# Local attention layers: where the shifted copies of the values are issued, and which engine writes their column of ones

## The chip, the core and the metric

The kernel runs on one core of a Trainium2 chip. Five engines are named in what follows: TensorE (PE for its matmuls, PEld for its weight loads), VectorE (DVE), ScalarE (ACT), GpSimd (POOL), and SyncE (SP), which here does nothing but issue DMAs, in the order of the program. The metric is the time of one execution on the device in microseconds (us).

## What is computed

A small transformer over x of 4 x 512 x 128: cross-attention and feed-forward layers before and after, and between them a stack of six local layers, which is where the change lies. One of them, cut to what matters:

```python
qkv = x @ Wqkv                       # 16 heads of 64
q = l2norm(q) * qs; k = l2norm(k) * ksc
q = q * cos * scale + rotate_half(q) * sin * scale      # k with 1 / scale
# windows of 32 rows: each looks at its own 32 keys and the 32 before
bk2 = concatenate([previous window of k, window of k])
bv2 = concatenate([previous window of v, window of v])
sim = q @ bk2.T * 8, masked to the 33 keys i-32 .. i
out = softmax(sim) @ bv2
x = out @ Wo + x
x = feed_forward(shift_tokens(x)) + x
```

## The kernel before

**Tiles and periods.** The local stack (`local_transformer`) works on tiles of 128 tokens: 6 layers x 4 rows x 4 tiles = 96 tiles. One loop, `for n in range(len(tiles) + 2)`, runs over periods. The order of every engine's instructions is that of the program (a manual schedule), and in period n three tiles are in work: T = tile n (its queries, keys and values), T1 = tile n-1 (transposes, scores, softmax) and T2 = tile n-2 (average, output projection). Every four periods a row of the feed-forward layer is woven in as well, in four phases.

The order within a period, with the lines that the profile names:

1. At n = 7, 23, 39, 55, 71 the next layer's weights are loaded: twelve DMAs on SP (`local_columns` L1757 to L1761, `local_weights` L1769 to L1781). At n = 4, once, two buffers in HBM are cleared for the last layer: POOL fills a tile (L527, L528), then SP issues three DMAs (L533 twice, L537), some 2 MB each.
2. Products of queries and keys on TensorE (L1842), their squares on ScalarE (L1844); `rotate` on VectorE (L1852, L1855, and the sum of squares L1864), with an addition on POOL (L1865). Between them the transposes of T2's probabilities (L621, copied by L1970), the first feed-forward part (L2017, L2028, L2039), the averages of T2 (`average`, L1980, twice), T1's transposes (L621, L1896), and T2's division (L1989, L1990).
3. The scores of T1 (L1940, L1949).
4. The last `rotate`; `normalise` of T on POOL (L1875 to L1884, the last of which are four products of 128x512); `softmax` of T1: row maxima on VectorE (L1959), subtraction (L1960), exponential on ScalarE (L1965).
5. The output projection of T2 (L2004) and the residual (L2011); in the first feed-forward phase the layer norm on VectorE (`ff_norm`, L559), whose result L2028 transposes in the next period.
6. `values` of T: products (L1919), copied to `v1` by ScalarE (L1920).
7. The second feed-forward part (L2039, L2050, L2062).

**v1 and v2.** `average` multiplies with 65 columns: 64 values and a column of ones that gives the sum of the probabilities. A window's 64 keys are its own 32 and the 32 before; windows of odd number find them as 64 neighbouring partitions of `v1`, those of even number in `v2`, a copy of `v1` shifted by 32 partitions (`x0` tells even and odd heads, whose halves lie swapped). Six DMAs within SBUF make `v2` (L1922 to L1930; four for the first tile of a row, whose missing part POOL sets to zero at L1915, L1916); two of them take rows of the tile before. The DMAs move the column of ones too, so they stand behind the memset that writes it, L1913 on POOL, which in POOL's order stands behind the four products of `normalise`. `v1` and `v2` have three buffers each.

In period n the copies of tile n go out; `average` reads them in period n+2.

Of the kernel before, what the change touches and what calls it, by code (L numbers as in the profile page):

```python
# [35 lines left out]
DEPTH, LH, LD, WIN = 6, 16, 64, 32  # L36
# [87 lines left out]
def bc(ap, shape, *axes):  # L124

    for a in axes:
        ap = ap.unsqueeze(a)
    return ap.to_broadcast(shape)
# [144 lines left out]
def tile_kernel(ctx: ExitStack, tc: tile.TileContext, A: dict, out: bass.AP):  # L273
    nc = tc.nc
    V, G, SC, PE, DMA = nc.vector, nc.gpsimd, nc.scalar, nc.tensor, nc.sync
# [43 lines left out]
    def p_tr(*shape):  # L319
        return psum(shape, "tr", 2)  # L320
# [199 lines left out]
    def clear(pool, i):  # L520


        t = pool.tile([128, NT, D], F32, name="xn")
        t = t.rearrange("p a b -> p (a b)")[:, : 2 * ROW].rearrange("p (a b) -> p a b", b=ROW)

        def fill(e):
            e.memset(t, 0.0)  # L527
            e.memset(t[:, 1, D + 1 :], NOWHERE)  # L528

        def send(e):  # L530
            for j in (1, 2) if i else (0,):
                r = sent[j].rearrange("(c p) d -> p c d", p=128)
                e.dma_start(r, bc(t[:, int(j != 1)], [128, r.shape[1], ROW], 1))  # L533

        def send_back(e):
            r = back[i].rearrange("(c p) d -> p c d", p=128)
            e.dma_start(r, bc(t[:, 0, :D], [128, 2 * NTT, D], 1))  # L537

        return fill, send, send_back
# [1211 lines left out]
    def local_columns(i, wp):  # L1751

        W = A["L2_ffn_Wqkv"][i]
        w = []
        for j in range(4):
            t = wp.tile([128, 512], F32, name="wqk", bufs=8)
            DMA.dma_start(t, W[:, 512 * j : 512 * j + 512])  # L1757
            w.append(t)
        qs = wp.tile([128, 2, LD], F32, name="qs", bufs=1)
        DMA.dma_start(qs[:, 0], A["L2_ffn_q_scale"][i].partition_broadcast(128))  # L1760
        DMA.dma_start(qs[:, 1], A["L2_ffn_k_scale"][i].partition_broadcast(128))  # L1761
        return w, qs

    def local_weights(i, wp, lf):

        W = A["L2_ffn_Wqkv"][i]
        wv = wp.tile([128, 2, 512], F32, name="wv")
        for x0 in range(2):
            DMA.dma_start(  # L1769
                wv[:, x0].rearrange("p (k d) -> p k d", d=LD),  # L1770
                W[:, 2 * INNER :].rearrange("p (k x d) -> p x k d", x=2, d=LD)[:, x0],
            )
        wo = wp.tile([128, 8, D], F32, name="wo")
        DMA.dma_start(wo, A["L2_ffn_Wo"][i].rearrange("(c p) d -> p c d", p=128))
        w1 = lf.tile([128, 2 * DI], F32, name="lw1")
        DMA.dma_start(w1, A["L2_ffn_W1"][i])
        w2 = lf.tile([128, 3, D], F32, name="lw2")
        DMA.dma_start(
            w2[:, 0:2], A["L2_ffn_W2"][i][0:256].rearrange("(c p) d -> p c d", p=128)
        )  # L1780
        DMA.dma_start(w2[: CH_W[2], 2], A["L2_ffn_W2"][i][256:DI])  # L1781
        return wv, wo, w1, w2
# [21 lines left out]
    def local_transformer(Y, lf, lw, columns, tabs):  # L1804

        with ExitStack() as es:
# [98 lines left out]
            def values(T, x0):  # L1905

                b, tt = T.b, T.tt
                if x0 == 0:  # L1910
                    T.v1 = vp.tile([128, 2, LH // 2, LD + 1], F32, name="v1")
                    T.v2 = vp.tile([128, 2, LH // 2, LD + 1], F32, name="v2")
                    G.memset(T.v1[:, :, :, LD : LD + 1], 1.0)  # L1913
                    if tt == 0:
                        G.memset(T.v2[0:32, 0], 0.0)  # L1915
                        G.memset(T.v2[64:96, 1], 0.0)  # L1916
                t = p_tr(128, 8, LD)
                src = Y[b] if x0 == 0 else swapped[b]
                PE.matmul(t, src[:, 128 * tt : 128 * tt + 128], T.wv[:, x0], start=True, stop=True)  # L1919
                SC.copy(T.v1[:, x0, :, 0:LD], t)  # L1920
                if x0 == 0:
                    DMA.dma_start(T.v2[32:128, 0], T.v1[0:96, 0])  # L1922
                    if tt:
                        DMA.dma_start(T.v2[0:32, 0], T.before.v1[96:128, 0])
                else:
                    DMA.dma_start(T.v2[96:128, 1], T.v1[64:96, 1])
                    DMA.dma_start(T.v2[0:32, 1], T.v1[96:128, 1])
                    DMA.dma_start(T.v2[32:64, 1], T.v1[0:32, 1])
                    if tt:
                        DMA.dma_start(T.v2[64:96, 1], T.before.v1[32:64, 1])  # L1930

            def scores(T):

# [21 lines left out]
            def softmax(T):  # L1955

                P = tp.tile([128, LH // 2, 2, LD], F32, name="P", bufs=1)
                mx = small.tile([128, 2, LH // 2], F32, name="la_mx")
                V.tensor_reduce(mx, T.banks, AX.X, ALU.max)  # L1959
                V.tensor_tensor(  # L1960
                    P.rearrange("p k z d -> p z k d"), T.banks,
                    bc(mx, [128, 2, LH // 2, LD], 3), ALU.subtract,
                )
                T.P = P.rearrange("p k z d -> p k (z d)")
                SC.activation(T.P, T.P, AF.Exp, scale=8.0)  # L1965

            def probabilities(T):
                T.PT = tp.tile([128, LH // 2, 128], F32, name="PT", bufs=1)
                for g in range(2):
                    SC.copy(T.PT[:, 4 * g : 4 * g + 4], to_features(T.P[:, 4 * g : 4 * g + 4]))  # L1970
# [51 lines left out]
            def ff_norm(F):  # L2022
                layernorm(F.xn, F.xn, F.found)
# [71 lines left out]
            for n in range(len(tiles) + 2):  # L2095
                T = tiles[n] if n < len(tiles) else None
                T1 = tiles[n - 1] if 0 <= n - 1 < len(tiles) else None
                T2 = tiles[n - 2] if 0 <= n - 2 < len(tiles) else None
                m, phase = divmod(n - 6, 4)
                F = rows[m] if 0 <= m < len(rows) else None  # L2100
                if T:
                    if n % 16 == 7 and T.i + 1 < DEPTH:
                        columns[T.i + 1] = local_columns(T.i + 1, lw)
                        loaded[T.i + 1] = local_weights(T.i + 1, wp, lf)
                    if n == 4:
                        fill, send, send_back = clear(lnp, 1)
                        fill(G)
                        send(DMA)
                        send_back(DMA)
                    if n % 16 == 15 and T.i + 1 < DEPTH:  # L2110
                        tabs[T.i + 1] = local_tables(columns[T.i + 1][1], lw)
                    T.before = tiles[n - 1] if T.tt else None
                    T.w, (T.wv, T.wo) = columns[T.i][0], loaded[T.i][:2]
                    T.tabs = tabs[T.i]
                    queries_or_keys(T, 0, 0)
                if T2:
                    probabilities(T2)
                if T:
                    queries_or_keys(T, 0, 1)
                    rotate(T, 0, 0)  # L2120
                if F:
                    ff_stage(F, phase, False)
                if T2:
                    average(T2, 0)
                if T1:
                    turned(T1, 0)
                if T:
                    queries_or_keys(T, 1, 0)
                if T2:
                    normalised(T2, 0)  # L2130
                if T:
                    rotate(T, 0, 1)
                if T2:
                    average(T2, 1)
                if T1:
                    turned(T1, 1)
                if T:
                    queries_or_keys(T, 1, 1)
                if T2:
                    normalised(T2, 1)  # L2140
                if T:
                    rotate(T, 1, 0)
                if T2:
                    attended(T2)
                if T and T.tt == NT - 1 and n + 1 < len(tiles):
                    swap(tiles[n + 1].b)
                if T1:
                    scores(T1)
                if T:
                    rotate(T, 1, 1)  # L2150
                if T:
                    normalise(T)
                if T1:
                    softmax(T1)
                if T2:
                    project_out(T2)
                    residual(T2)
                if F and phase == 0:
                    ff_norm(F)
                if T:  # L2160
                    values(T, 0)
                    values(T, 1)
                if F:
                    ff_stage(F, phase, True)
# [134 lines left out]
```

## Time and profile before

| | us |
|---|---|
| three runs, median | 2462.2 (2459.23 to 2467.07) |
| the profiled execution | 2456.04 |
| its span | 2454.2 |
| local layers, within the span (first and last average) | 545 to 2164 |
| TensorE busy | 2228.0 |
| VectorE busy | 1759.3 |
| GpSimd busy | 1338.6 |
| ScalarE busy | 1298.1 |

All statements of durations come from the profiled execution; 1.8 us of its time lie outside the span. Rows of a timeline have the start and the duration in us, the engine, the line, the operation and what it writes and reads; a bracket at the end has the engine's idle time before it and what ended it. SPq is SP's queue, where the duration is that of issuing, not of the transfer. A busy TensorE isn't a TensorE at its peak, and what an engine waits for is inferred from semaphores.

### The profile page before, as it was taken

The numbers are of one execution on the slowest core, as the hardware profiler recorded it, in microseconds if no ns is written. First come the engines' busy times: TensorE is split into PE (matmuls) and PEld (weight loads), VectorE is DVE, ScalarE is ACT, GpSimd is POOL, SyncE is SP. The second block draws the span as 40 slices with busy tenths as digits, with TensorE's granted clock in tenths as the row PEclk, the third lists the DMA queues.
The fourth block names the chain that finished last, engine by engine and source line by source line (L and its number), as shares of the span: only waits on it lengthen the run. The fifth ranks groups of instructions, "written<-read, shape, count | busy, mean of one in ns | idle before, by whom it ended". The sixth has DMA issues, their size and how long they took to land. (4 is left out here: it accounts for less than half of the span.)

```text
span 2454.2 us, 86703 instructions
## 1 busy us (share of the span) xinstructions
PE 2228.0 (91%) x37341; PEld 1479.5 (60%) x37341; DVE 1759.3 (72%) x3896; ACT 1298.1 (53%) x2389; POOL 1338.6 (55%) x1862
## 2 busy tenths in 40 slices
PE   7958969978999999999999999999999999989676
PEld 3536734546666666666666666666666666644355
DVE  5545356866888888777887888887878788767422
ACT  3423325645666655666666666565666666525222
POOL 2141330256667676766667766766667666710433
PEclk9868989988999999999999999999999999989688
DMA  7201110016211121111211121111211111120023
GB/s 182 68 21 41 40 60 2 1 41 135 80 35 29 35 70 36 33 29 35 75 31 36 29 79 33 29 35 27 80 31 31 35 29 35 27 67 23 26 67 95
DMA packets 134298, 116.14 MB, mean 47 GB/s; under 512 B 29506, under 2 KB 102701, under 8 KB 133917
## 3 DMA queue, kind: packets, MB, share of 16 engines
q1 hardware_dynamic: 122037, 99.67, 15.8%
q0 software_dynamic: 4608, 7.35, 0.9%
q8 instruction: 296, 4.85, 0.9%
q10 hardware_dynamic: 7271, 3.58, 0.5%
q14 instruction: 86, 0.70, 0.1%
HBM read 42.84 MB, written 21.52 MB: 26 GB/s over the span
## 5 line engine op out<-in xcount | busy, mean ns | idle before, releaser
L1865 POOL TENSOR_TENSOR rc<-rc,rs 128x512 f32<-128x512 f32 x384 | 489.8, 1276 | 400.7 <-DVE rs L1855 326.3
L1842 PE MATMUL ps_mm<-wqk,y 128*128 128x512 f32 x768 | 397.2, 599 | 5.3 <-issue 3.5
L1884 POOL TENSOR_TENSOR rc<-rc,rn_y 128x512 f32<-128x512 f32 x384 | 388.6, 1044 | 7.5
L1852 DVE TENSOR_TENSOR rc<-ps_mm,tabs 128x512 f32<-128x512 f32 x384 | 262.5, 684 | 129.8 <-ACT sq L1844 126.5
L1844 ACT ACTIVATE sq<-ps_mm 128x512 f32<-128x512 f32 x384 | 231.2, 602 | 161.4 <-PE ps_mm L1842 108.0
L1855 DVE TENSOR_TENSOR rs<-ps_mm,tabs 128x512 f32<-128x512 f32 x384 | 261.5, 681 | 0.2 <-POOL rc L1865 0.2
L1864 DVE TENSOR_REDUCE ss<-sq 128x8 f32<-128x512 f32 x384 | 259.5, 676 | 0.0
L621 PE MATMUL ps_tr<-cst,rc 128*128 128x128 f32 x1536 | 210.9, 280 | 4.3 <-POOL rc L1884 4.0
L1980 PEld LDWEIGHTS ps_av<-v,PT 64*32 64x32 f32 x12288 | 138.1, 105 | 126.5 <-PE ps_tr L621 54.1
L2004 PE MATMUL ps_av<-aT,wo 128*128 128x128 f32 x1536 | 200.7, 283 | 2.4 <-issue 2.4
L2004 PEld LDWEIGHTS ps_av<-aT,wo 128*128 128x128 f32 x1536 | 181.0, 193 | 12.6 <-issue 3.9
L621 PEld LDWEIGHTS ps_tr<-cst,rc 128*128 128x128 f32 x1536 | 165.6, 142 | 24.4 <-POOL rc L1884 5.1
L1949 PE MATMUL ps_sc<-kT,qT 64*32 64x64 f32 x12288 | 148.1, 225 | 33.6 <-issue 32.9
L1980 PE MATMUL ps_av<-v,PT 64*32 64x65 f32 x12288 | 170.3, 225 | 6.2 <-DVE attn L1990 1.7
L1949 PEld LDWEIGHTS ps_sc<-kT,qT 64*32 64x32 f32 x12288 | 141.2, 105 | 44.2 <-issue 38.1
L1056 POOL DMA_INDIRECT back<-ye,to x80 | 78.8, 985 | 147.5 <-DVE ye L1170 104.0
L1842 PEld LDWEIGHTS ps_mm<-wqk,y 128*128 128x128 f32 x768 | 124.5, 192 | 56.3 <-issue 50.1
L1965 ACT ACTIVATE P<-P 128x1024 f32<-128x1024 f32 x96 | 101.4, 1057 | 97.3 <-DVE P L1960 97.3
L1876 ACT ACTIVATE rn_y<-ss 128x32 f32<-128x32 f32 x96 | 22.0, 229 | 237.9 <-POOL ss L1875 237.9
L802 ACT ACTIVATE P<-ps,deltaT 77x512 f32<-77x512 f32 x192 | 115.8, 683 | 56.7 <-PE ps L796 53.0
L1896 ACT COPY qT<-ps_tr 128x512 f32<-128x512 f32 x192 | 103.3, 589 | 74.6 <-PE ps_tr L621 74.3
L1959 DVE TENSOR_REDUCE la_mx<-ps_sc 128x16 f32<-128x1024 f32 x96 | 116.9, 1218 | 31.0 <-PE ps_sc L1949 31.0
(399 smaller groups left out, 4368.9 us busy)
## 6 DMA issues: line engine op xcount, KB each, us to landing
v<-v SPq DMA_DIRECT2D x432, 65.0 KB
v<-v SPq DMA_DIRECT2D x96, 195.0 KB
wqk<-in_L_ffn_Wqkv_dram SPq DMA_DIRECT2D x24, 256.0 KB
sent<-xn SPq DMA_DIRECT2D x2, 2210.0 KB
xe<-sent SPq DMA_DIRECT2D x16, 260.0 KB
back<-xn SPq DMA_DIRECT2D x2, 2048.0 KB
raw<-in_L_ffn_W_dram SPq DMA_DIRECT2D x8, 512.0 KB
w<-in_L_ffn_W_dram SPq DMA_DIRECT2D x16, 256.0 KB
```

Source lines behind the costliest of these rows:

```text
L621: PE.transpose(t[:, i], src[:, i], ident)
L1842: PE.matmul(t, lhs, T.w[2 * kind + c], start=True, stop=True)
L1844: SC.activation(sq, t, AF.Square)
L1852: V.tensor_tensor(a, t, bc(T.tabs[:, 2 * kind, tt], [128, 8, LD], 1), ALU.mult)
L1855: V.tensor_tensor(r.rearrange("p h (x d) -> p h x d", x=2), t.rearrange("p h (x d) -> p h x d", x=2)[:, :, ::-1], bc(T.tabs[:, 2 * kind + ...
L1864: V.tensor_reduce(T.ss[:, kind, 8 * c : 8 * c + 8], sq, AX.X, ALU.add)
L1865: G.tensor_tensor(a, a, r, ALU.add)
L1884: G.tensor_tensor(a, a, bc(y[:, o : o + 8], [128, 8, LD], 2), ALU.mult)
L1949: PE.matmul(T.banks[32 * w : 32 * w + 32, z, k], T.qT[r, k, 32 * w : 32 * w + 32], T.kT[r, k, 32 * w : 32 * w + 64], start=False, stop=Tru ...
L1959: V.tensor_reduce(mx, T.banks, AX.X, ALU.max)
L1980: PE.matmul(T.means[32 * w : 32 * w + 32, x0, k], T.PT[r, 4 * g + k, 32 * w : 32 * w + 32], (T.v1 if w % 2 else T.v2)[r, x0, 4 * g + k], s ...
L2004: PE.matmul(t, T.wo[:, c], T.aT[:, c], start=(c == 0), stop=(c == 7))
```

## The change

The function `ship` takes the six DMAs out of `values`, and in front of them the column of ones is written by VectorE instead of POOL. It is called for T1 just ahead of its `softmax`: the copies of tile n now go out in period n+1, in step 4 above. `average` still reads them in period n+2. On VectorE the memset stands behind the last `rotate` and ahead of the row maxima. On SP the copies of tile n-1 now stand behind the DMAs that step 1 of period n issues. Shapes and transfers are the same.

```diff
@@ values(T, x0)
                 if x0 == 0:
                     T.v1 = vp.tile([128, 2, LH // 2, LD + 1], F32, name="v1")
                     T.v2 = vp.tile([128, 2, LH // 2, LD + 1], F32, name="v2")
-                    G.memset(T.v1[:, :, :, LD : LD + 1], 1.0)
                     if tt == 0:
                         G.memset(T.v2[0:32, 0], 0.0)
                         G.memset(T.v2[64:96, 1], 0.0)
...
                 SC.copy(T.v1[:, x0, :, 0:LD], t)
-                if x0 == 0:
-                    DMA.dma_start(T.v2[32:128, 0], T.v1[0:96, 0])
-                    if tt:
-                        DMA.dma_start(T.v2[0:32, 0], T.before.v1[96:128, 0])
-                else:
-                    DMA.dma_start(T.v2[96:128, 1], T.v1[64:96, 1])
-                    DMA.dma_start(T.v2[0:32, 1], T.v1[96:128, 1])
-                    DMA.dma_start(T.v2[32:64, 1], T.v1[0:32, 1])
-                    if tt:
-                        DMA.dma_start(T.v2[64:96, 1], T.before.v1[32:64, 1])
+            def ship(T):
+
+                v1, v2 = T.v1, T.v2
+                before = T.before.v1 if T.tt else None
+                V.memset(v1[:, :, :, LD : LD + 1], 1.0)
+                DMA.dma_start(v2[32:128, 0], v1[0:96, 0])
+                if T.tt:
+                    DMA.dma_start(v2[0:32, 0], before[96:128, 0])
+                DMA.dma_start(v2[96:128, 1], v1[64:96, 1])
+                DMA.dma_start(v2[0:32, 1], v1[96:128, 1])
+                DMA.dma_start(v2[32:64, 1], v1[0:32, 1])
+                if T.tt:
+                    DMA.dma_start(v2[64:96, 1], before[32:64, 1])
@@ the loop over periods
                 if T:
                     normalise(T)
                 if T1:
+                    ship(T1)
                     softmax(T1)
                 if T2:
                     project_out(T2)
```

## The prediction

> **What bounds the kernel now.** I read the page first, then the local stretch alone, then who waits in it, then one period of the loop, and last the one place where the sync queue (SP) carries something big.
>
> ```profile
> PE 2228.0 (91%) x37341; PEld 1479.5 (60%) x37341; DVE 1759.3 (72%) x3896; ACT 1298.1 (53%) x2389; POOL 1338.6 (55%) x1862
> PE   7958969978999999999999999999999999989676
> 700.00:2100.00 1400.00, 1360.74 (x27239) 923.36 (x27239) 1140.44 (x1991) 857.36 (x1565) 957.02 (x1344) 1.00 0.15 40
> PE ps_sc L1949 <- issue: 26.1, 26, 1.5
> PE ps_tr L621 <- ACT v L1920: 3.4, 12, 0.3
> PE ps_sc L2028 <- DVE xn L559: 3.0, 8, 0.5
> ```
>
> Lines one and two are the page's; the third is the window table (us, then busy time of PE, PEld, DVE, ACT, POOL, clock, DMA share, GB/s); the last three are TensorE's waits in that window (total us, times, longest). TensorE is busy 1360.7 of 1400 us, and two thirds of the 39 us that are missing are "issue" before the scores, which no engine and no copy ends. No wait on the copies of v appears. So nothing that is merely taken off POOL or SP can help; what can happen is a new wait. One period lasts about 17 us (82 row maxima, L1959, in 1400 us).
>
> **How much room the copies have.** Timeline of a period with the least room, and a set of copies:
>
> ```profile
> 1030.62 0.68 DVE L1864 TENSOR_REDUCE ss<-sq 128x8 f32<-128x512 f32 x1
> 1031.21 1.22 DVE L1959 TENSOR_REDUCE la_mx<-ps_sc 128x16 f32<-128x1024 f32 x1
> ...
> 1037.96 1.02 PE L1980 MATMUL ps_av<-v,PT 64*32 64x65 f32 x64
> ...
> 1038.51 0.13 POOL L1913 MEMSET v<- 128x16 f32 x1
> 1038.66 0.53 SPq L1922 DMA_DIRECT2D v<-v  x1
> ```
>
> Now the copies of tile n go out behind POOL's memset at 1038.66, and are read over a period later. After the change they go out just before L1959 of the next period (1031.21 here), and the average L1980 at 1037.96 reads them: 6.75 us. What a set needs: from the first issue at 1019.33 to the last, L1930, 1022.47 + 0.59 = 1023.06, that is 3.73 us of issuing; the window table has the DMA share at 0.05 in 1024.0 to 1024.5 and 0.00 after, so 5.2 us at most. The slowest ordinary set, from 1038.66, still moves in 1044 to 1045: 6.3 us. Other tiles have 8 to 10 us (1013.16 to 1022.35, 1047.46 to 1056.22). So ordinary copies arrive in time, with 0.4 to 1.5 us to spare in every fourth tile. I cost this at nothing; the upper end is 24 tiles x 0.5 us = 12.
>
> **The SP queue that the copies are moved past.** SP works in order. At 7, 23, 39, 55 and 71, weight loads stand at the head of a period, and at 4 the clearing of the buffers in HBM (L533, L537). Today both stand behind the copies that are next needed; afterwards the copies of tile n-1 stand behind them.
>
> ```profile
> 579.16 0.59 SPq L1930 DMA_DIRECT2D v<-v  x1
> 579.86 8.05 SPq L533 DMA_DIRECT2D sent<-xn  x2
> 587.96 12.94 SPq L537 DMA_DIRECT2D back<-xn  x1
> 601.01 9.16 SPq L1922 DMA_DIRECT2D v<-v  x1
> ...
> 588.53 0.42 PE L1980 MATMUL ps_av<-v,PT 64*32 64x65 f32 x21
> 597.60 1.22 PE L1842 MATMUL ps_mm<-wqk,y 128*128 128x512 f32 x1 [3.50 <-issue]
> ```
>
> ```profile
> 588.00:596.00 8.00, 5.76 (x149) 3.62 (x147) 6.77 (x13) 3.83 (x7) 6.71 (x9) 1.00 1.27 190
> 596.00:604.00 8.00, 5.49 (x127) 4.01 (x128) 1.88 (x3) 2.23 (x5) 2.40 (x6) 0.55 1.29 180
> 604.00:610.00 6.00, 3.92 (x34) 3.74 (x34) 2.45 (x2) 0.78 (x1) 4.59 (x7) 0.50 1.14 306
> ```
>
> The clearing holds SP and all DMA engines from 579.86 to 610.17 (601.01 + 9.16, when the copy behind it was taken). It already costs something: TensorE waits for instructions, its clock falls to 0.5, and the row maxima of tiles 3 and 4 lie 24.2 us apart (582.50, 606.70). The L1930 above is tile 3's, and tile 3 is averaged at 588.53.
>
> **Part by part.**
>
> *Clearing, once.* Afterwards tile 3's six copies are issued in period 4 behind the clearing. SP gets to it when POOL's fill ends (L528, 575.34) less the memset that goes, 0.13: 575.21, that is 4.65 us earlier than 579.86. The first copy is then taken at 610.17 - 4.65 = 605.52; five more take 3.73 - 0.53 = 3.2; the last lands 1.0 to 1.4 us after its issue (1023.06 to 1024.0 or 1024.5): 610.0. The average that ran at 588.53 waits until then: 21.5 us of new wait on TensorE, with everything else of the period queued behind it. Average to maxima took 8.11 us in the period before (574.39 to 582.50). The clock will be low after such a gap: at best nothing is lost, at worst all 8.11 us of it run at half speed; in the rows it stayed near 0.5 from 596.8 to 610.4 after a gap of 3.5 us, but with gaps inside. I take 2.5 us. The maxima of tile 4 come at 610.0 + 8.1 + 2.5 = 620.6 instead of 606.70. Part comes back: the instruction starvation is hidden in the wait (counted already, since 606.70 holds it), and the next period, 17.30 us (606.70 to 624.00), holds a slow L2004 (3.78 us where 2.05 is usual), 1.7 us. I take half of that: 16.5. So 637.1 against 624.00: **+13.1 us**; ends +9.7 (no cold loss, all 1.7 back, 609.6) and +18.
>
> The Trainium skill, "TensorE: Matmul & The Clock Gate", Part 1, says that the array is cold after an idle window of about 3.4 us and warm again after about 3.4 us of steady work. By that rule the cold loss would be about 1.7 us instead of my 2.5, and the sum 0.8 us lower; the 13.6 us at 0.5 in this trace had further gaps in them.
>
> *Weight loads, five times.* Their issues take 635.91 to 645.74. Afterwards they start when tile 5's copies are issued (maxima at 624.00, so near 628) and are issued by 638, before the maxima of tile 6 at 640.27: the copies find SP free. Zero, up to 1 us each; 0 to +5.
>
> *Ones on VectorE.* VectorE's memsets cost 60 ns for 77x2 (L658) and 485 ns for 128x512 (L654), on one line with 16 elements at 72 ns: 96 x 0.072 = 6.9 us. It stands behind L1864 and ahead of L1959; behind it wait the maxima, the subtraction, the residual and, every fourth period, the norm L559, on which TensorE's L2028 waits. In 30 of 96 periods VectorE waits for the scores anyway (31.0 us). Where TensorE waits for VectorE's chain it is one period in four: 24 x 0.072 = **+1.7 us**; elsewhere TensorE's own work covers it.
>
> A worse price is possible: L559 beside POOL's L1884 takes 957 ns, the same kind of operation and size (L588) 348. If POOL's addition L1865, in flight at that moment, held the memset as well, it would be 0.6 us each, 14 us in 24 periods, 58 in all. Rows L654 and L658 are memsets and read nothing; I take them.
>
> The Trainium skill, "SBUF — State Buffer", "Who interferes with whom", lists copies, casts and tensor_scalar as holders of the port that VectorE shares with GpSimd, and says that an instruction with at most one SBUF input outside those modes doesn't contend. By it the memset pays nothing extra, and the 0.6 us would be no case at all; no row here has a VectorE memset beside a busy POOL.
>
> *Removed from POOL.* 96 x 128 ns = 12.3 us, behind the norm's four products and ahead of L1865, which waits 326 us for VectorE anyway; nothing waits on POOL's memset but SP. Zero.
>
> *DMA out of the averages' way.* TensorE's "issue" waits at L1980 and L621 are 1.6 us in the window: 0 to -2; I take 0.
>
> Sum: 13.1 + 1.7 = **+14.8 us**, on the profiled execution's 2456.04: 2470.8. The three runs' median is 6.2 us higher, 2462.2, so I forecast 2477.0. A change under 0.3% (7.4 us) can't be told from none here.
>
> **Rivals.**
> 1. *The clearing is hidden (not slower).* The present kernel loses 7 us there already; if the copies land soon enough, the wait only replaces that. With tile 3's copies landing at 597 instead of 610 the 13.1 is gone. For it: the clearing's first two transfers are issued in 8 us. Against: L1922 sat 9.16 us. Time 2462 to 2466. Chance 0.13.
> 2. *Copies late throughout, or a memset that blocks.* 24 tiles x 0.5 = 12, or 24 x 0.6 = 14, weights 5: +27 to +32 in all, 2489 to 2494. For it: a margin of 0.4 us; against: rows above. Chance 0.17.
> 3. *Faster.* If the "issue" gaps before the scores (26.1 in 1400, 30 in the whole stage) were due to the copies' packets, their going would outweigh the clearing: 14.8 - 30 = -15, 2447. It decides from about 15 us saved. Against: the packets are over by 1024.5 and the scores run at 1029. Chance 0.06.
> 4. *Nothing moves*, because the copies still go out as before: impossible to see in the rows; in 1.
>
> Forecast 0.64. Slower by over 0.3%: 0.64 + 0.17 = 0.81; within: 0.13; faster: 0.06. The range goes from 2464 (rival 1, upper part) to 2494 (rival 2).
>
> **What will show it.** Right: L1980 with one wait of some 20 us on a DMA of v near 588, tile 3's L1922 behind L537, maxima of tiles 3 and 4 some 38 us apart, MEMSET on DVE near 72 ns, no other DMA wait in 700 to 2100. Wrong: L1980 waiting in many periods, a MEMSET far over 0.1 us, or less "issue" time before L1949.

## The result, and the profile after

Five runs of the changed kernel have a median of 2486.8 us (2484.0 to 2488.7) against 2462.2 us before: a ratio of 1.0098, with a 95% interval of 1.0082 to 1.0114. The change makes the kernel 24.6 us slower; the forecast was 14.8 us slower, within a range that holds the measured time. The profiled execution took 2484.23 us, its span 2482.2.

TensorE's line and its slices on the page after:

```profile
PE 2236.2 (90%) x37341; PEld 1483.3 (60%) x37341; DVE 1761.5 (71%) x3992; ACT 1297.6 (52%) x2389; POOL 1330.6 (54%) x1766
PE   7958969977999999999999999999999999989676
```

TensorE does the same work, with one slice at 7 where there was an 8. TensorE's waits after, in 560 to 2164 us (total us, times, longest):

```profile
PE ps_sc L1951 <- issue: 36.0, 31, 3.1
PE ps_av L1982 <- DMA v<-v: 15.1, 2, 14.9
PE ps_av L1982 <- issue: 6.2, 5, 2.2
PE ps_tr L621 <- POOL kT L1892: 2.2, 1, 2.2
```

and the same before:

```profile
PE ps_sc L1949 <- issue: 32.9, 31, 2.2
PE ps_av L1980 <- issue: 1.7, 4, 0.6
```

(In the kernel after, the scores L1949 are L1951, the averages L1980 L1982, the maxima L1959 L1961, and the copies L1925 to L1932.) Two things are new and recur below: one wait of 14.9 us for a copy of v, and waits for instructions ("issue") at the averages. The single wait of 2.2 us at L621, put down to POOL, lies in the fifth weight load (at 1749.92 us).

The plainest ruler is the row maxima, one per tile: they give the length of every step. In the table, "all" runs from the maxima of tile 0 to those of tile 95, "2 to 5" covers the clearing, "5 to 6" is the sum of the five steps between tiles 5 and 6 of layers 0 to 4 (the steps after which the next layer's weights must be under way), and "rest" is what remains. Each figure is a difference of starts of that line in one profiled execution, in us.

| | all | 2 to 5 | 5 to 6, five | rest |
|---|---|---|---|---|
| before | 1615.4 | 56.5 | 80.5 | 1478.4 |
| after | 1636.0 | 67.5 | 93.3 | 1475.2 |

The stage is 20.6 us longer: 11.0 at the clearing, 12.8 at the five weight loads, and -3.2 in the 87 steps of the rest. In this pair of profiles another 7.4 us lie outside the stage, where the instructions are the same. That part moves from one execution to the next: the maxima of tile 0 came at 515.0, 515.7 and 518.6 us in three profiles of the experiments below, whose programs don't differ before them. 20.6 us is inside the interval of the runs (20.2 to 28.1 us).

Each figure of the table comes from one profile of each kernel, and such a figure moves too. Up to tile 5, experiment 4 below runs the same program as the kernel before and takes 51.9 us from tile 2 to 5 instead of 56.5; experiment 1 runs the same as the kernel after and takes 64.1 instead of 67.5. So the clearing's cost is 8 to 16 us, 11.0 in this pair. The rest lies between 1471.8 and 1481.3 us in all profiles but those of experiments 7 and 8, so its -3.2 is no change that can be told from none.

**The clearing.** SP and TensorE after (timeline; SPq durations are of issuing):

```profile
576.17 0.59 SPq L1932 DMA_DIRECT2D v<-v  x1
580.48 7.79 SPq L533 DMA_DIRECT2D sent<-xn  x2
588.32 12.43 SPq L537 DMA_DIRECT2D back<-xn  x1
600.86 8.76 SPq L1925 DMA_DIRECT2D v<-v  x1
...
589.85 0.97 PE L1951 MATMUL ps_sc<-kT,qT 64*32 64x64 f32 x72 [3.06 <-issue]
590.75 3.34 PE L2006 MATMUL ps_av<-aT,wo 128*128 128x128 f32 x16
613.61 0.39 PE L1982 MATMUL ps_av<-v,PT 64*32 64x65 f32 x2 [14.85 <-DMA v<-v]
```

Tile 3's first copy is taken at 600.86 + 8.76 = 609.62, its last is issued at 612.21, and the average that reads them starts at 613.61 after a wait of 14.85 us. The scores ahead of it have already waited 3.06 us for instructions, and L2006 runs at half clock (3.34 us where it takes 2.05; the window table reads 0.50 for 592 to 594 us).

**The weight loads.** The step from tile 21 to tile 22, after:

```profile
915.93 1.20 DVE L1961 TENSOR_REDUCE la_mx<-ps_sc 128x16 f32<-128x1024 f32 x1
919.85 2.04 SPq L1757 DMA_DIRECT2D wqk<-in_L_ffn_Wqkv_dram  x4
927.81 0.33 PE L1982 MATMUL ps_av<-v,PT 64*32 64x65 f32 x12 [1.57 <-issue]
928.65 0.36 SPq L1781 DMA_DIRECT2D lw<-in_L_ffn_W_dram  x1
933.93 0.65 PE L1951 MATMUL ps_sc<-kT,qT 64*32 64x64 f32 x40 [1.79 <-issue]
```

and before:

```profile
897.21 1.22 DVE L1959 TENSOR_REDUCE la_mx<-ps_sc 128x16 f32<-128x1024 f32 x1
906.78 0.86 PE L1980 MATMUL ps_av<-v,PT 64*32 64x65 f32 x64
908.68 2.56 SPq L1757 DMA_DIRECT2D wqk<-in_L_ffn_Wqkv_dram  x4
910.56 1.46 PE L1949 MATMUL ps_sc<-kT,qT 64*32 64x64 f32 x128
917.59 0.36 SPq L1781 DMA_DIRECT2D lw<-in_L_ffn_W_dram  x1
```

Before, the loads start 11.5 us after the maxima, when both averages are done, and the scores pass whole 2 us later. After, they start 3.9 us after the maxima; 6 us into them the second average breaks off for 1.57 us, and 12 us after their start the scores for 1.79. Both waits are "issue", that is, for nothing that the profile names; in each a 16 KB packet of code begins 2.3 to 2.5 us before TensorE goes on, and I read them as TensorE lacking its own instructions. The second wait outlasts the load: the DMA share is 0.63 in 931 to 932 us and 0.00 in 932 to 934. Over the five steps TensorE stands idle for 17.3 us, where it was 6.5 before, and in the first of them it also runs at half clock for 3 us; together this is nearly all of the 12.8 us.

**The memset.** VectorE's rows at the same place after:

```profile
915.32 0.68 DVE L1864 TENSOR_REDUCE ss<-sq 128x8 f32<-128x512 f32 x1
915.93 1.20 DVE L1961 TENSOR_REDUCE la_mx<-ps_sc 128x16 f32<-128x1024 f32 x1
915.96 0.07 DVE L1924 MEMSET v<- 128x16 f32 x1
```

All 96 take 72 ns, as forecast, although POOL's addition L1865 is in flight beside 95 of them (915.54 to 916.81 here). The recorded memset lies inside the row of the maxima here.

### The profile page after: what moved, and what is told of

It is laid out like the page before. It is cut to its first block, busy times and chain, and to the rows that moved or that the text cites. A ratio compares the mean times of both kernels' runs of the same rounds, so it can differ in the third digit from the quotient of the medians.

```text
span 2482.2 us, 86795 instructions
## 1 busy us (share of the span) xinstructions
PE 2236.2 (90%) x37341; PEld 1483.3 (60%) x37341; DVE 1761.5 (71%) x3992; ACT 1297.6 (52%) x2389; POOL 1330.6 (54%) x1766
## 4 chain that ended last, share of the span: by engine, by line
PE 69%; DVE 13%; issue 9%; DMA 3%; ACT 2%; POOL 2%; SPq 1%; another core or an unknown queue 1%; DVEq 0%; POOLq 0%; ACTq 0%
PE ps_tr L621 12%; PE ps_mm L1842 11%; PE ps_av L2006 6%; PE ps_av L1982 5%; PE ps_tr L1918 5%; PE ps_sc L1951 4%; PE ps_sc L2052 2%; PE ps_sc L2064 2%; PE ps_sc L2041 2%; DVE xn L559 2%; PE ps L812 1%; PE ps L821 1%; PE ps L1610 1%; DVE rc L1852 1%; PE ps L1717 1%
## 5 line engine op out<-in xcount | busy, mean ns | idle before, releaser
L1865 POOL TENSOR_TENSOR rc<-rc,rs 128x512 f32<-128x512 f32 x384 | 489.0, 1274 | 429.0 <-DVE rs L1855 389.8
L1864 DVE TENSOR_REDUCE ss<-sq 128x8 f32<-128x512 f32 x384 | 259.4, 675 | 0.0
L1982 PEld LDWEIGHTS ps_av<-v,PT 64*32 64x32 f32 x12288 | 137.8, 105 | 146.9 <-PE ps_tr L621 53.4
L621 PE MATMUL ps_tr<-cst,rc 128*128 128x128 f32 x1536 | 212.4, 282 | 6.0 <-POOL rc L1884 3.9
L2006 PE MATMUL ps_av<-aT,wo 128*128 128x128 f32 x1536 | 200.0, 283 | 1.9 <-issue 1.9
L1982 PE MATMUL ps_av<-v,PT 64*32 64x65 f32 x12288 | 170.3, 225 | 25.9 <-DMA v<-v 15.1
L2006 PEld LDWEIGHTS ps_av<-aT,wo 128*128 128x128 f32 x1536 | 180.6, 192 | 11.7 <-issue 3.0
L621 PEld LDWEIGHTS ps_tr<-cst,rc 128*128 128x128 f32 x1536 | 166.7, 142 | 26.4 <-POOL rc L1884 5.1
L1951 PE MATMUL ps_sc<-kT,qT 64*32 64x64 f32 x12288 | 147.6, 224 | 37.0 <-issue 36.0
L1951 PEld LDWEIGHTS ps_sc<-kT,qT 64*32 64x32 f32 x12288 | 140.6, 105 | 47.3 <-issue 41.0
L1842 PEld LDWEIGHTS ps_mm<-wqk,y 128*128 128x128 f32 x768 | 124.8, 193 | 52.2 <-issue 45.8
L1896 ACT COPY qT<-ps_tr 128x512 f32<-128x512 f32 x192 | 103.4, 589 | 90.8 <-PE ps_tr L621 90.6
L1896 ACT COPY kT<-ps_tr 128x512 f32<-128x512 f32 x192 | 103.4, 590 | 72.4 <-PE ps_tr L621 72.1
```

Source lines behind the costliest of these rows:

```text
L621: PE.transpose(t[:, i], src[:, i], ident)
L1842: PE.matmul(t, lhs, T.w[2 * kind + c], start=True, stop=True)
L1864: V.tensor_reduce(T.ss[:, kind, 8 * c : 8 * c + 8], sq, AX.X, ALU.add)
L1865: G.tensor_tensor(a, a, r, ALU.add)
L1896: SC.copy(t[:, 4 * c : 4 * c + 4, lead:], to_features(T.rot[kind, c].rearrange("p (k x) d -> p k (x d)", x=2)),)
L1951: PE.matmul(T.banks[32 * w : 32 * w + 32, z, k], T.qT[r, k, 32 * w : 32 * w + 32], T.kT[r, k, 32 * w : 32 * w + 64], start=False, stop=Tru ...
```

## The experiments

My theory after the result was that the change costs two episodes and nothing in an ordinary period: the clearing, behind which tile 3's copies stand, and the weight loads, which start earlier in the period because SP reaches them earlier and then starve TensorE of instructions. The rival was that every period pays, through the memset on VectorE or copies that come late throughout. The kernels of the first four experiments ran together, the next four together, and the last two together, each group on another chip; ratios are to the kernel before on the same chip, where its median was 2412.5, 2420.6 and 2456.9 us. Lengths of steps come from one profile of each kernel and are compared with the two profiles above. The chips differ mostly outside the local stage: the maxima of tile 0 come at 514 to 519 us in the first group and at 538 to 544 in the last, and what follows those of tile 95 takes 276 to 283 and 300 us.

**1. Loads held back by POOL** (a one-column write of the first weight tile, at the head of the period):

```diff
 t = wp.tile([128, 512], F32, name="wqk", bufs=8)
+if gate and not j:
+    gate.memset(t[:, 0:1], 0.0)
 DMA.dma_start(t, W[:, 512 * j : 512 * j + 512])
...
-columns[T.i + 1] = local_columns(T.i + 1, lw)
+columns[T.i + 1] = local_columns(T.i + 1, lw, G)
```

Expected:

> The changed kernel, with the weight loads of the five layers held back: POOL writes one column of the first weight tile at the head of periods 7, 23, 39, 55, 71, so that SP can't start the loads before POOL is through with the norm of the tile before, which is the time at which they start in the kernel before. Theory 'two episodes' (the clearing once, and five weight loads that start some 8 us earlier in the period and starve TensorE of instructions): the five steps seen in the profile after (2.9, 3.4, 2.4, 1.4, 2.7 us between the row maxima of tiles 5 and 6 of a layer, 12.8 in all) go, 2486.8 - 12.8 = 2474 us, and the 'issue' waits of 1 to 2 us at the second average and the scores of those periods go back to one of about 1 us. Rival 'every period pays' (the memset on VectorE or copies that come late throughout): no change, 2487.

Measured: 1.0078 (1.0049 to 1.0107). The five steps take 90.6 us, and the five after them 88.2 where they took 83.6 before: nothing is gained. The edit missed its aim: POOL is through 7.4 us after the maxima, but in the kernel before the loads also stand behind four microseconds of copies and start 11.5 to 12 us after them. The scores of those periods now wait 1.9 to 4.0 us instead of the averages. So holding them back by half the way is as bad, and neither theory is decided.

**2. The clearing in pieces:**

```diff
-fill, send, send_back = clear(lnp, 1)
-fill(G)
-send(DMA)
-send_back(DMA)
+pieces = clear_pieces(vp)          # the same rows, three times 128 at a time
...
 if T1:
     ship(T1)
     softmax(T1)
+if 4 <= n:
+    next(pieces, None)
```

> The changed kernel, with the three clearing DMAs of period 4 cut into 35 pieces of some 190 KB, one behind each tile's copies in periods 4 to 38; the source of the zeros gets a tile of its own. Theory 'two episodes': tile 3's copies no longer stand behind 30 us of clearing, and the loss that the kernel before has there goes as well; the row maxima of tiles 3 and 4 come 17 us apart instead of 33.8 in the profile after: -11 for the change's part (what is left of it at tile 5) and -7 for the old part, 2486.8 - 18 = 2469 us. Rival 'every period pays': 2486.8 - 7 to 2486.8. If the pieces themselves cost, up to 35 x 0.3 = 10 of it comes back.

Measured: 1.0008 (0.9989 to 1.0026). Tiles 2 to 5 take 45.3 us instead of 67.5; the wait of an average on a copy is gone. That is 22 us for the clearing alone, of which 11 came with the change and 11 were lost before as well. The loads' five steps stay at 96.2.

**3. Both:**

> The changed kernel with both: the weight loads held back by POOL's one column, and the clearing in 35 pieces. Theory 'two episodes': 2486.8 - 12.8 - 18 = 2456 us, which is 6 us below the kernel before, since the old loss at the clearing is gone as well. Rival 'every period pays': 2480 or more; what is left above 2455 would be the price of the memset on VectorE and of the later copies (forecast 1.7 us).

Measured: 0.9991 (0.9971 to 1.0010). The gain came 4 us short of the theory's (2 us below the kernel before instead of 6). The held-back loads still cost 15.0 us (89.3 in the five steps and 89.8 in the five after them, against 80.5 and 83.6), where the theory had them gone; the clearing gave back more than forecast (44.3 us for tiles 2 to 5).

**4. The kernel before, its loads alone moved early:**

```diff
-if n % 16 == 7 and T.i + 1 < DEPTH:
-    columns[T.i + 1] = local_columns(T.i + 1, lw)
-    loaded[T.i + 1] = local_weights(T.i + 1, wp, lf)
...
     residual(T2)
+if T and n % 16 == 6 and T.i + 1 < DEPTH:
+    columns[T.i + 1] = local_columns(T.i + 1, lw, V)     # V writes one column first
+    loaded[T.i + 1] = local_weights(T.i + 1, wp, lf)
```

> The kernel before, with copies and column of ones as they were, and one thing alone moved: the weight loads are issued one period earlier, behind a one-column write of VectorE that stands behind the residual, some 3 us after the row maxima of tile 5 of a layer (in the profile after they start 4 us after them). Theory 'two episodes': the time of the loads within the period is what costs, so + 12.8 us, 2462.2 + 12.8 = 2475, with 'issue' waits at the second average and at the scores of those periods. Rival (the loads only hurt together with the later copies, which share the DMA engines with them): no change, 2462.

Measured: 1.0050 (1.0029 to 1.0070), 12 us. The five steps take 95.5 us, 15.0 more than before, with copies and ones where they always were:

```profile
871.74 1.22 DVE L1961 TENSOR_REDUCE la_mx<-ps_sc 128x16 f32<-128x1024 f32 x1
874.86 1.78 SPq L1759 DMA_DIRECT2D wqk<-in_L_ffn_Wqkv_dram  x4
884.50 0.46 PE L1982 MATMUL ps_av<-v,PT 64*32 64x65 f32 x12 [2.40 <-issue]
```

It is the timeline of its step from tile 21 to tile 22: the loads start 3.1 us after the maxima, and the second average breaks off at the same place as in the changed kernel. Starting the loads at this place is enough; the rival, that they hurt only beside the later copies, falls.

**5. The changed kernel, clearing in pieces and loads in five groups**, one behind the copies of each of five tiles:

```diff
+def issue():
+
+    if queue:
+        for dst, src in queue.pop(0):
+            DMA.dma_start(dst, src)
...
-DMA.dma_start(t, W[:, 512 * j : 512 * j + 512])
+later(j // 2, t, W[:, 512 * j : 512 * j + 512])       # and so on: qs and wv 2, wo 3, w1 and w2 4
...
     softmax(T1)
+issue()
```

> The changed kernel with the clearing in 35 pieces and the weight loads of each layer in five groups, one behind the copies of each of five tiles from period 7 on, instead of twelve in a row. Theory (a load of 9 to 10 us that starts 4 to 8 us after the row maxima starves TensorE of instructions at the next average and the next scores; groups of 2 to 3 us are over before those need their code): the steps of tiles 5 to 6 go from 18.0 to 19.2 us each (93 in all) to about 16 (80), and with the clearing spread the whole local stage takes some 1602 us where the kernel before takes 1615 and the changed one 1636: 13 us below the kernel before, ratio 0.995. Rival (the bytes of the loads cost the same wherever they lie, or the later copies and the memset on VectorE cost something in every period): no better than with the clearing in pieces and the loads held back, ratio 0.999.

Measured: 0.9940 (0.9922 to 0.9958), 14.5 us below the kernel before and faster than both kernels. The stage takes 1600.1 us, with 45.8 at the clearing and 79.2 in the five steps. Its rest is 1475.1 us, which is the changed kernel's 1475.2 and 3 us below the 1478.4 of before: with the two episodes gone, no cost of later copies or of a memset on VectorE is to be seen. TensorE's waits, in the same window as above:

```profile
PE ps_sc L1982 <- issue: 25.7, 28, 1.4
PE ps_av L2013 <- issue: 1.6, 4, 0.6
```

(L1982 are the scores here, L2013 the averages.) The waits at the averages are back at what they were before, and no copy is waited for.

**6. The kernel before, clearing in pieces** (the edit of 2, behind `values`):

> The kernel before, with the clearing of period 4 in 35 pieces behind the copies of periods 4 to 38, and nothing else. Theory: the kernel before loses time there too; its steps between tiles 3, 4 and 5 (24.2 and 17.3 us) go to 15 and 15.5: -11 us, ratio 0.9955. Rival (the pieces cost elsewhere what they save): ratio 0.999 to 1.000.

Measured: 0.9965 (0.9947 to 0.9982), 8.5 us. Tiles 2 to 5 go from 56.5 to 46.0 us: the old loss was real. Of this, 3.0 us come back in the five steps of the loads (83.5) and 2.9 in the rest, both within what moves from profile to profile.

**7. The kernel before, pieces and groups:**

> The kernel before, with the clearing in pieces and the weight loads in five groups as well. Theory: the loads cost nothing at their place in the kernel before (steps of tiles 5 to 6: 80.5 us for five), so the groups bring nothing beyond the pieces: -11 us, ratio 0.9955; if the copies' place makes no difference once nothing big shares the queue, this and the changed kernel with the same two edits take the same time within 2 us, except for the memset on VectorE. Rival: the groups bring another 1 us or more for each of five layers here as well, ratio 0.993.

Measured: 0.9990 (0.9972 to 1.0009). A miss: the groups lose what the pieces gain. Most of the loss lies in the step from tile 8 to tile 9, in which the third group (the scales and `wv`) goes out: the five take 101.8 us, against 93.7 with pieces alone, and the scores of each wait 2.1 to 3.5 us for instructions instead of 1.0 to 1.4. In this kernel a group stands behind `values`, and this one starts 10.8 to 12.5 us after the maxima; in the changed kernel groups stand behind `softmax`, and it starts 2.7 to 3.3 us after them. The groups have another place in the two kernels, so whether the copies' own new place matters here is not shown. And the whole load of the kernel before starts 11.5 to 12.0 us after the maxima of tile 5 without such a loss: the time since the maxima alone doesn't decide what a load costs.

**8. The kernel before, with five more memsets on VectorE:**

```diff
 if T1:
+    for _ in range(5):
+        V.memset(extra[:, :, :, LD : LD + 1], 1.0)
     softmax(T1)
```

> The kernel before, with five more memsets of the same shape (128x16, one column of ones each, into a tile that nobody reads) on VectorE ahead of the row maxima of every period: 5 x 72 ns = 0.36 us. Nothing is left out. My theory (it shows only where TensorE waits for VectorE's chain, one period in four): 24 x 0.36 = 8.6 us, ratio 1.0035. Rival one (every period pays): 96 x 0.36 = 35 us, ratio 1.014. Rival two (TensorE's own work covers all of it): ratio 1.000, and the single memset of the change is then free. Rival three (POOL's addition in flight holds the memsets): rows of MEMSET on DVE far above 72 ns.

Measured: 1.0136 (1.0111 to 1.0160), 33 us: the figure of rival one, but not its way. VectorE's rows around the maxima of tile 21:

```profile
893.71 0.68 DVE L1864 TENSOR_REDUCE ss<-sq 128x8 f32<-128x512 f32 x1
894.36 0.54 DVE L2156 MEMSET extra<- 128x16 f32 x4
894.95 1.20 DVE L1959 TENSOR_REDUCE la_mx<-ps_sc 128x16 f32<-128x1024 f32 x1
894.98 0.07 DVE L2156 MEMSET extra<- 128x16 f32 x1
```

From the start of L1864 to that of the maxima are 1.24 us, against 0.59 before (the row shown in the prediction) and 0.61 (915.32 to 915.93) in the changed kernel. Five memsets into one tile start 154 ns apart (why not closer is not shown): they cost 0.65 us a period, while the single one costs about 0.02. By the position of the tile in its row the steps grow by a median of -0.08, 0.67, 0.63 and 0.11 us: two steps of four pay all of it, two none. My "one period in four" was wrong, and so was the price: 0.13 us for each of five in place of 0.072, and 0.02 for a single one. The experiment overstates what the change's one memset costs.

**9. The change with its column of ones left on POOL:**

```diff
-V.memset(v1[:, :, :, LD : LD + 1], 1.0)                 # in ship
+G.memset(T.v1[:, :, :, LD : LD + 1], 1.0)               # in values, as before
```

> The change without its memset on VectorE: the column of ones is written by POOL where the kernel before writes it, and the copies stand in program order where the change puts them. Nothing then holds a tile's copies until the next softmax except SP's order, so they go out when POOL's memset is through, 7.4 us after the row maxima, as before; but the weight loads and the clearing still stand ahead of the copies of the tile before. Theory: the loads, which follow tile 5's copies at once, start some 5 us ahead of the next maxima, at the place in the period that cost nothing before; so the 12.8 us of the loads go, and the clearing's 11 stay: before + 11 to 12, ratio 1.0045 to 1.005, with tile 3's average still waiting some 15 us on its copies. Rival (the order on SP alone is the whole of it): ratio 1.010. Second rival (the clearing's wait needs VectorE's late memset too): ratio 1.000.

Measured: 1.0053 (1.0035 to 1.0071), 13 us. The five steps take 82.9 us, the four steps before them in layers 1 to 4 (tiles 4 to 5) 75.0 instead of 73.7, tiles 2 to 5 64.3 (8 over before), and tile 3's average waits 14.5 us on its copies. So the change has two halves: the order on SP makes the clearing's cost, and the wait for VectorE's memset makes that of the loads. SP and the maxima around tile 21 here:

```profile
898.65 0.59 SPq L1932 DMA_DIRECT2D v<-v  x1
899.28 2.04 SPq L1757 DMA_DIRECT2D wqk<-in_L_ffn_Wqkv_dram  x4
909.81 0.36 SPq L1781 DMA_DIRECT2D lw<-in_L_ffn_W_dram  x1
...
907.89 1.22 DVE L1961 TENSOR_REDUCE la_mx<-ps_sc 128x16 f32<-128x1024 f32 x1 [0.66 <-PE ps_sc L1951]
```

Tile 21's copies and the loads behind them go out before tile 21's maxima, 8.6 us ahead of them: late in the period, where they cost little (2.4 us in the five steps and 1.3 in the four).

**10. The clearing behind tile 3's copies instead of ahead of them:**

```diff
 if n == 4:
     fill, send, send_back = clear(lnp, 1)
     fill(G)
-    send(DMA)
-    send_back(DMA)
...
     ship(T1)
     softmax(T1)
+if n == 4:
+    send(DMA)
+    send_back(DMA)
```

> The changed kernel with the three clearing DMAs issued behind tile 3's copies (after its softmax in period 4) instead of ahead of them. Theory (a set of copies has under 10 us of room, so whichever set stands behind 30 us of clearing is late): tile 3 is in time, and the next set, tile 4's, waits instead, 13 to 15 us at its average; the whole within 4 us of the changed kernel, ratio 1.008 to 1.0115. Rival (it was only tile 3's place): the 11 us go, ratio 1.0055.

Measured: 1.0049 (1.0027 to 1.0072). A miss: the wait does move to tile 4's copies, but it is 4.6 us and not 13 to 15. Tiles 2 to 5 take 59.5 us, 3.0 over the kernel before. Tile 4 is the first of a row, has four copies instead of six, and its average would be later anyway, because the scores ahead of it have been starved (4.1 us). The rival's forecast, 1.0055, was nearer: most of the clearing's cost hangs on its standing ahead of tile 3's copies, which are needed within the period.

## Why the prediction was right, point by point, and where it was short

- *TensorE is the bound, and only new waits can matter*: right. The rest of the steps did not grow (1478.4 and 1475.2 us).
- *Ordinary copies arrive in time*: right. No average outside the clearing waits for a copy, neither after nor in experiment 5.
- *The clearing, +13.1*: the mechanism and nearly the size: +12.8 at the maxima of tile 4, counted from those of tile 0, and +11.0 at tile 5. Its parts were less good than their sum. With 5.4 us taken off, by which this execution began its stage later, the average starts at 608.2 us (forecast 610.0), but reaches its place only at 593.4 (613.61 - 14.85 - 5.4) and not at 588.5, after starved and slow scores: hence a wait of 14.85 us and not 21.5. The next step gave back 1.8 us, as in the forecast's best case. The forecast's ends were not worked out alike: with the landing at 609.6 that it names, the lower is +9.3 and not +9.7, and the upper, +18, takes the worst clock together with all 1.7 us given back; with none given back it is +19.5. The measured 11.0 lies within either.
- *The cold clock, 2.5 us*: right. From the average to the maxima of tile 4 it takes 11.28 us (613.61 to 624.89) instead of 8.11; 0.75 of the 3.2 us are short waits (0.28 and 0.47). The window table after (the column behind the five busy times is the granted clock) shows TensorE cold for some 5 us of work, not for the 13.6 us of the trace of before, which had gaps in them:

```profile
613.00:616.00 3.00, 2.11 (x67) 1.72 (x68) 0.35 (x2) 0.00 (x0) 0.00 (x0) 0.50 0.15 38
616.00:618.00 2.00, 2.00 (x8) 1.61 (x8) 2.00 (x4) 1.07 (x2) 0.11 (x1) 0.50 0.00 0
618.00:620.00 2.00, 2.00 (x69) 1.03 (x68) 0.55 (x2) 0.70 (x2) 1.42 (x2) 0.86 0.00 0
```

  The Trainium skill ("TensorE: Matmul & The Clock Gate", Part 1) puts it at about 3.4 us of sustained work; after this wait it was some 5 us, with short gaps in them, and the measurement decides.
- *Weight loads, zero, at most +5*: **this is the step that failed**. I asked only whether SP would be free for the copies; it is. I didn't ask what the loads do to TensorE at the new place in the period, although the clearing's rows in the prediction show TensorE waiting 3.50 us for instructions beside a large transfer. They took 12.8 us; experiment 4 shows 12 us from moving them alone, experiment 9 that without the late memset they cost 3.7 (2.4 and 1.3), and experiment 5 that behind `softmax` in groups they cost nothing.
- *Ones on VectorE, +1.7*: a duration of 72 ns as forecast, a price of about 0.02 us a period, no effect to be seen. The rival that POOL would hold the memset is out: 72 ns in all 96.
- *POOL's memset gone, zero*: right. POOL's waits for VectorE at L1865 grew, from 326.3 to 389.8 us.
- *Rival 1 (clearing hidden)* failed: the clearing cost 11.0 us; *rival 3 (faster)*: the "issue" waits before the scores stayed (32.9 and 36.0 us), so the copies at their old place didn't make them.
- *The range*: its upper end, 2494 us, was rival 2's (copies late throughout, or a memset that blocks), and neither came about. That the range still holds 2486.8 owes something to luck: the loads, costed at nothing, filled the room that rival 2 had made.

Together 11.0 + 12.8 = 23.8 us less 3.2 in the rest, against 14.8 forecast.

What stays open is why an instruction wait grows with the time since a load began. The trace has 16 KB packets of code beside the loads; in the waits of the loads, as in the ordinary ones before the scores, TensorE goes on 2.3 to 2.9 us after such a packet begins, and the packets themselves take about 1 us as always. So what is late is the start of the packet and not its transfer. That the load's packets stand ahead of it is argued from the experiments that move the loads, and is not shown; nor is why the third group of experiment 7 costs what it does.

## What to carry to other kernels

A DMA that is moved within a program moves everything behind it on its queue: list what else the queue carries, and ask of each when it will now start and which engine is in its densest code at that time. A load of 10 us was free 11.5 us after the row maxima and cost 2.6 us when it began 4 us after them; cut into groups of 0.6 to 2.7 us of issuing, behind the copies of the changed kernel, it was free. Cutting the clearing into pieces made the kernel before 0.35% faster by itself; cutting its loads as well lost that again (experiment 7), while in the changed kernel the same two cuts give a time 0.6% below the kernel before. So try large transfers in pieces, and measure the place of the pieces as well.

## What the runs showed of the hardware that was not expected

- A VectorE memset of 16 elements between a reduction and the row maxima cost 0.02 us here, not its 72 ns (0.61 us from the one to the other instead of 0.59); five into the same tile cost 0.65 us, 154 ns from start to start.
- TensorE ran short of instructions beside large transfers: not at 2 us into a load (before, tile 22), for 1.6 us at 6 us into it and for 1.8 at 12 us, when it had just ended (after, tile 22), for up to 4.0 us in experiment 1 and 3.1 us under the clearing.
- Such a wait can cost more than itself: after one of 2.2 us (up to 652.67, in the step to tile 6) the window table reads 0.50 as the granted clock for 653 to 656 us.
